# Attention and mixture of experts on one core: the last sequence's exponentials go by HBM, and one unit of shared-expert work moves ahead of the last router

## The chip, the cores and the metric

The kernel runs on one core of a Trainium2 chip. Its metric is the device time of one execution in microseconds (us). Five engines work side by side, each through a queue of its own in a fixed order: TensorE (PE, matmuls and transposes), VectorE (DVE), ScalarE (ACT), GpSimd (POOL) and SyncE (SP, which issues transfers here). An instruction waits until the semaphores that it names have arrived; everything behind it in its queue waits with it. Transfers (DMA) run on 16 DMA engines that all queues share.

## The reference, cut to what matters

Eight sequences of 512 tokens with 256 features, all in float32:

```python
x = x + attention(layernorm(x))          # causal, one head of 256, 8 sequences of 512
h = layernorm(x)
shared = (silu(h @ shared_gate) * (h @ shared_up)) @ shared_down        # inner size 512
probs = sigmoid(h @ router_w.T + routing_bias)                          # 8 experts
scores, indices = top_k(probs, 2); scores /= scores.sum(-1)
for each token and each of its two experts e:
    combined += score * ((silu(h @ gate_w[e]) * (h @ up_w[e])) @ down_w[e])
x = x + shared + combined
```

Each token goes to two of eight experts, so 8192 rows of expert work have to be sorted by expert at run time. No expert tile can start before the last sequence has been routed.

## The kernel before, in words

**Three phases.** The first phase walks over the eight sequences, numbered 0 to 7, and does attention, the second norm and the router for each. The second phase works through the routed rows in tiles of 256 (later 128) rows, each with one expert's weights. The third does the shared expert of sequences 4 to 6, which the first phase left over, and adds everything up.

**Attention of a sequence.** A sequence has four chunks of 128 tokens (`NT = 4`). `scores` (line 437) makes one chunk's masked scores and its exponentials. `attend` (line 458) multiplies the turned exponentials with the values: one matmul for chunk 0, two for chunk 1, three for chunk 2, four for chunk 3. The sums go into PSUM tiles called `av`, DVE adds them to the residual (line 476), takes the statistics (line 172), POOL raises the variance to the power of -1/2 (line 179), and DVE writes the normalized row `hn` (line 325). The pool `ps_o` holds `av` and also the small results of the router (`lT`, `pl`), of the placing (`pp`) and of the shared expert's second layer (`po`). It has two buffers, so each of these waits until the one before the last has been read.

**Two ways to turn a tile.** The exponentials must be turned before the second matmul. Sequences in `SENT` (1 to 6) take the way by HBM: all four chunks' scores are made ahead, at the end of the sequence before; two DMAs store the exponentials, eight load them as 32x32 squares (line 424), and DVE turns these (line 434) into `exTs`, first the tile of chunks 0 to 2 (128x768), then that of chunk 3 (128x512). Sequences 0 and 7 take the other way: scores chunk by chunk inside the attention, and PE transposes (line 463) with ACT copies (line 465). The normalized rows for the router have the same two ways: sequences in `WHOLE` (1 to 5) go by HBM in two halves (lines 371, 377, 384); sequence 7 is in `VIA` but not in `WHOLE`, so its first half goes by HBM and its second by PE (line 340); sequences 0 and 6 go by PE.

**Units.** A shared-expert unit (`shared_beside`, line 564) is half a sequence: four hidden blocks of two matmul groups each (line 578, 16 matmuls), ACT's tanh (line 589), two DVE products for each block (lines 593, 596), and eight matmuls of the second layer (line 605). The list `waiting` holds eight units of sequences 0 to 3, and two of sequence 7 at the end. One unit stands beside each of the sequences 0 to 5, after the next sequence's scores and values; the router of that sequence runs inside it. None stands beside sequence 6, whose router runs at once. One unit is interleaved with sequence 7's attention and router (the call with `halfway=mixed`): its blocks 0 and 1 may go before that attention's last matmul, the others after. Three units are left behind the last router.

**The tail of the first phase.** The router's logits (`lT`, line 492) become probabilities and choices on DVE (lines 504 to 535), `places_of` (line 540) turns them into row numbers `at`, and POOL sends each chunk's rows to HBM by indirect DMA (`dispatch`, line 557, eight DMAs for one sequence). `plan_tiles` (line 189) makes the table of tiles and writes blank rows (line 199). Then SP loads the first tile's rows `h` (line 851), which wait for every dispatched row and blank, DVE turns them into `hTt` (line 873), and PE starts the first expert tile (line 900). ACT issues the expert weights `w` (line 838).

**What sets the order.** The program is written once, in the order that the loops have it; a scheduler then lays out each engine's queue. `tc.issue_after(x)` makes what it holds stand behind `x` where both are on the same engine; it adds no wait. Within these rules the scheduler puts first what it holds to be ready first, and the built queue is fixed from then on.

Of the kernel before, what the change touches and what calls it, by code (L numbers as in the profile page):

```python
# [26 lines left out]
def kernel(  # L27
# [248 lines left out]
    with ExitStack() as first, ExitStack() as inner:  # L276
# [181 lines left out]
        def attend(xb, i, ex, inv, v, mv, rstd, hn, meanwhile=None, exT=None):  # L458
            n = (i + 1) * P
            if exT is None:  # L460
                pt = ps_t.tile([P, S], F32, tag="t", name="pt")
                for j in range(i + 1):
                    nc.tensor.transpose(pt[:, ts(j, P)], ex[:, ts(j, P)], ident)
                exT = work.tile([P, S], F32, tag="exT", name="exT")
                marks["exT"] = nc.scalar.copy(exT[:, :n], pt[:, :n]).ins
            else:
                exT = part(exT, i)
            if meanwhile is not None:
                meanwhile()
            av = ps_o.tile([P, D], F32, tag="o", name="av")  # L470
            for j in range(i + 1):
                mixed = nc.tensor.matmul(  # L472
                    av, lhsT=exT[:, ts(j, P)], rhs=v[:, j, :], start=(j == 0), stop=(j == i)
                )
            with tc.issue_after(marks["turned"]) if "turned" in marks else nullcontext():
                summed = nc.vector.scalar_tensor_tensor(
                    out=xb[:, i, :], in0=av, scalar=inv, in1=xb[:, i, :], op0=ALU.mult, op1=ALU.add
                )
            stats_of(mv, xb[:, i, :], i)
            power = rstd_of(rstd[:, i : i + 1], mv[:, i : i + 1, :])  # L480
            if i:
                with tc.issue_after(summed.ins) if i != NT // 2 or xb is not total[B - 1] else nullcontext():
                    normalize(hn[:, i - 1, :D], xb, i - 1, mv, rstd)
            return mixed.ins, summed.ins, power

        def route(b, hT, hn):
# [22 lines left out]
            for r in range(TOP):  # L509
                top, hot = tops[r][:, here], hots[r][:, here, :]  # L510
                if r:
                    yield
                with tc.issue_after(marks["turned"]) if r and b < B - 2 else nullcontext():
                    nc.vector.tensor_reduce(out=top, in_=prob, axis=AX.X, op=ALU.max)
                nc.vector.tensor_tensor(
                    out=hot, in0=prob, in1=top.unsqueeze(2).to_broadcast(wide), op=ALU.is_equal
# [47 lines left out]
        def shared_beside(b, half, hT, midway=None, behind=None, rows_from=NI, early=None, steps=(), halfway=None):  # L564
# [8 lines left out]
            for m in range(NI):  # L573
                pg = ps_m.tile([P, 2, n], F32, tag="m", name="pg")
                for w in range(2):
# [13 lines left out]
                nc.scalar.activation(sg, pg[:, 0, :], AF.Tanh, scale=0.5)  # L589
# [40 lines left out]
        for b in range(B):  # L630
# [27 lines left out]
            for i in range(NT):  # L658
# [95 lines left out]
            def chosen(b=b, hT=hT, hn=hn):  # L754
# [18 lines left out]
            if b + 1 < B:  # L773
                choice = chosen()
                next(choice)
                if b + 2 == B:
                    for _ in choice:
                        pass
            else:
                added = shared_beside(*waiting.pop(0), early=chosen(), rows_from=0, halfway=mixed, steps=((NI // 2, 1), (NI - 1, 0), (NI - 1, 1)))  # L780
            if b in LATE:
# [3 lines left out]
                waiting += [(b, 0, hT), (b, 1, hT)]  # L785
            if b + 1 < B:

                if b + 2 < B:
                    def behind():

                        nonlocal exT
                        with tc.issue_after(marks["hid"]), tc.issue_after(marks["first"]):
                            exT = turn_exponentials(squares)
                        next(choice, None)
                        marks["squares"], marks["turned"] = marks["turned"], marks["run"]

                    def midway():
                        if b + 3 < B:
                            with tc.issue_after(marks["squares"]):
                                rows, _ = first_norm(*coming)  # L800
                            with tc.issue_after(marks["sent"]):
                                blocks[b + 3], _ = sent_to_blocks(xn_d[b + 3], rows)

                    added = shared_beside(
                        *waiting.pop(0), midway=midway, behind=behind, early=choice,
                        rows_from=1 if b in WHOLE else NI,
                        steps=((NI // 2, 1), (NI - 1, 1)) if b in WHOLE else ((0, 1), (1, 1)),
                    )
                xT = ahead_T
        placed()  # L810
        for c in to_send:
# [316 lines left out]
```

## Time and profile before

| what | value |
|---|---|
| median of 13 runs | 678.18 us (676.97 to 679.32) |
| the profiled execution's own time | 676.17 us |
| its span | 674.4 us |
| PE busy | 663.6 us, 98% of the span |
| DVE, ACT, POOL busy | 301.5, 151.0, 158.0 us |
| first expert matmul starts at | 259.26 us |
| PE's clock as granted | 1.00 in every stretch until PE has finished |

The span is what the profiler records; 1.8 us of the execution's time lie outside it. The median of the runs is 2.01 us above the profiled execution, so a sum made against the profile is carried over by adding 2.01 us.

The lines of a timeline are: start in us, time covered in us, engine, line of the kernel, operation, tile written <- tiles read, shape, and count. Behind them, in brackets, is how long the engine had been idle and what ended that. A float32 matmul counts as two instructions and a transpose by PE as one.

### The profile page before, as it was taken

To read this page: it belongs to the slowest core of one execution; us is meant where nothing else is said; L and a number is where in the kernel's file an instruction comes from. 1 tells how busy PE (TensorE), PEld (TensorE's weight loads), DVE (VectorE), ACT (ScalarE), POOL (GpSimd) and SP (SyncE) were. 2 spreads that over 40 slices of the span, in tenths; PEclk is the share of its full clock that TensorE was granted. 3 is DMA by queue.
4 is the path that set the end of the run, shared out by engine and by line. 5 is a ranking of instruction groups with operands and counts; after the bars stand their busy time and mean duration, and the time that the engine had idled before them with its cause. 6 is when DMAs were issued, how large, how long until landed. Compare 5 with 4: busy or idle time off the path is not lost.

```text
span 674.4 us, 10379 instructions
## 1 busy us (share of the span) xinstructions
PE 663.6 (98%) x3178; PEld 543.4 (81%) x3178; DVE 301.5 (45%) x1002; ACT 151.0 (22%) x359; POOL 158.0 (23%) x210
## 2 busy tenths in 40 slices
PE   7999999999999999999999999999999999999997
PEld 5677777777776888888888888888888899994556
DVE  4668879779776853212212122122122112223765
ACT  2442321332313222121111111211111111111110
POOL 3102451532516520112121111211121112121000
PEclk9999999999999999999999999999999999999999
DMA  7653877767743366967455454453543557824775
GB/s 229 185 140 108 227 211 188 209 185 219 210 120 128 108 174 216 274 175 218 140 174 163 127 181 137 152 180 111 172 160 106 165 164 237 246 91 154 245 222 176
DMA packets 152809, 118.48 MB, mean 176 GB/s; under 512 B 109648, under 2 KB 131280, under 8 KB 152752
## 3 DMA queue, kind: packets, MB, share of 16 engines
q1 hardware_dynamic: 133552, 57.00, 32.5%
q10 hardware_dynamic: 12912, 43.53, 18.6%
q0 software_dynamic: 6288, 17.24, 7.0%
q8 instruction: 28, 0.46, 0.3%
q14 instruction: 29, 0.24, 0.1%
HBM read 82.79 MB, written 34.95 MB: 175 GB/s over the span
## 4 chain that ended last, share of the span: by engine, by line
PE 94%; DVE 1%; DMA 1%; POOL 1%; ACTq 1%; ACT 1%; issue 1%; SPq 0%; DVEq 0%; POOLq 0%
PE po L923 17%; PE pg L900 17%; PE pu L900 17%; PE pg L578 10%; PE po L605 5%; PE av L472 4%; PE sc L442 4%; PE pm L395 4%; PE pm L407 4%; PE pg L1011 3%; PE po L1070 3%; PE pu L1011 3%; PE lT L492 1%; POOL rows_h L559 1%; DMA wk<-in_wk_dram 1%; ACTq L838 1%
## 5 line engine op out<-in xcount | busy, mean ns | idle before, releaser
L886 DVE TENSOR_TENSOR hidp<-pu,sgt 128x512 f32<-128x512 f32 x56 | 38.6, 690 | 209.9 <-PE pu L900 198.9
L929 POOL DMA_INDIRECT rows_y<-y,to x56 | 53.9, 962 | 266.2 <-ACT y L928 143.9
L900 PE MATMUL pg<-hTt,w 128*128 128x256 f32 x448 | 105.9, 379 | 0.1
L900 PE MATMUL pu<-hTt,w 128*128 128x256 f32 x448 | 105.8, 379 | 0.0
L923 PE MATMUL po<-w_down,hidp 128*128 x448 | 101.3, 379 | 0.0
L900 PEld LDWEIGHTS pg<-hTt,w 128*128 128x128 f32 x448 | 85.0, 190 | 12.0 <-ACT sgt L885 0.5
L900 PEld LDWEIGHTS pu<-hTt,w 128*128 128x128 f32 x448 | 85.1, 190 | 11.6
L923 PEld LDWEIGHTS po<-w_down,hidp 128*128 128x128 f32 x448 | 85.0, 190 | 11.5
L578 PE MATMUL pg<-hT,w_sh 128*128 128x256 f32 x320 | 74.0, 383 | 0.2 <-ACT hT L341 0.2
L559 POOL DMA_INDIRECT rows_h<-hn,at x64 | 63.4, 990 | 22.7 <-issue 17.5
L885 ACT ACTIVATE sgt<-pg 128x512 f32<-128x512 f32 x67 | 39.9, 597 | 127.6 <-PE pg L900 120.1
L578 PEld LDWEIGHTS pg<-hT,w_sh 128*128 128x128 f32 x320 | 59.5, 190 | 9.5 <-ACT sg L589 1.0
L928 ACT COPY y<-po 128x256 f32<-128x256 f32 x67 | 24.9, 373 | 150.6 <-PE po L923 145.9
L179 POOL TENSOR_TENSOR rstd<-var,minus_half 128x1 f32<-128x1 f32 (+1 forms) x43 | 27.0, 636 | 125.1 <-DVE var L178 94.2
L442 PE MATMUL sc<-xT,qT 128*128 128x128 f32 (+3 forms) x128 | 37.4, 434 | 0.0
L605 PE MATMUL po<-w_sh,hid 128*128 128x256 f32 x160 | 36.5, 381 | 0.0
L605 PEld LDWEIGHTS po<-w_sh,hid 128*128 128x128 f32 x160 | 29.5, 190 | 5.0 <-DVE hid L596 0.7
L395 PE MATMUL pm<-xT,w_qk 128*128 128x512 f32 x64 | 29.9, 592 | 0.0
L886 DVE TENSOR_TENSOR khid<-pu,sgt 128x512 f32<-128x512 f32 x11 | 7.6, 692 | 48.9 <-PE pu L900 48.9
L407 PE MATMUL pm<-wv_sb,xT 128*128 128x256 f32 x128 | 29.0, 380 | 0.2 <-ACT xT L341 0.2
L407 PEld LDWEIGHTS pm<-wv_sb,xT 128*128 128x128 f32 x128 | 24.2, 190 | 6.2 <-issue 2.6
L172 DVE BATCH_NORM_STATS2 bnst<-total 128x6 f32<-128x256 f32 x64 | 25.2, 410 | 8.1 <-DMA total<-in_x_dram 8.0
(156 smaller groups left out, 757.6 us busy)
## 6 DMA issues: line engine op xcount, KB each, us to landing
w<-in_gate_w_dram ACTq DMA_DIRECT2D x41, 512.0 KB, 3.9
w<-in_up_w_dram ACTq DMA_DIRECT2D x41, 512.0 KB, 4.3
yl<-rows_y SPq DMA_DIRECT2D x32, 256.0 KB, 3.9
h<-rows_h SPq DMA_DIRECT2D x112, 64.0 KB, 3.5
w_down<-in_down_w_dram SPq DMA_DIRECT2D x8, 512.0 KB, 5.3
out_dram<-total SPq DMA_DIRECT2D x32, 128.0 KB, 3.2
total<-in_x_dram SPq DMA_DIRECT2D x7, 512.0 KB
xnd<-xn SPq DMA_DIRECT2D x6, 512.0 KB
```

The source lines that it names most:

```text
L395: nc.tensor.matmul(pm, lhsT=w_qk[:, k, ts(m, P)], rhs=xT[:, k, :], start=(k == 0), stop=(k == ND - 1),)
L407: nc.tensor.matmul(pm, lhsT=xT[:, k, ts(c, P)], rhs=wv_sb[:, k, :], start=(k == 0), stop=(k == ND - 1),)
L442: nc.tensor.matmul(sc[:, :n], lhsT=qT[:, k, ts(i, P)], rhs=xT[:, k, :n], start=(k == 0), stop=(k == ND - 1),)
L559: lands(nc.gpsimd.indirect_dma_start(out=rows_h[:, :], out_offset=bass.IndirectOffsetOnAxis(ap=at[:, r, c : c + 1], axis=0), in_=hn[:, c, ...
L578: mm = nc.tensor.matmul(pg[:, w, :], lhsT=w_sh[:, ds(w * gu + k * I + m * P, P)], rhs=hT[:, k, at], start=(k == 0), stop=(k == ND - 1),)
L605: nc.tensor.matmul(po, lhsT=hid[:, m, ts(j, P)], rhs=w_sh[:, ds(2 * gu + m * D, D)], start=(m == 0), stop=(m == NI - 1),)
L885: nc.scalar.activation(sg, pg, AF.Silu)
L886: return nc.vector.tensor_tensor(out=hid, in0=pu, in1=sg, op=ALU.mult).ins
L900: nc.tensor.matmul(dst[:, m, :], lhsT=w[:, i, k, ts(m0 + m, P)], rhs=hT[:, ts(k, n * P)], start=(k == 0), stop=(k == ND - 1),)
L923: nc.tensor.matmul(po, lhsT=hid[:, m, ts(j, P)], rhs=w_down[:, ds(w + m * D, D)], start=(m == 0), stop=(m == NI - 1),)
L929: nc.gpsimd.indirect_dma_start(out=rows_y[:, :], out_offset=bass.IndirectOffsetOnAxis(ap=to[:, j : j + 1], axis=0), in_=y, in_offset=None,)
L1011: nc.tensor.matmul(dst, lhsT=w_sh[:, ds(off + k * I + m * P, P)], rhs=hT[:, k, :], start=(k == 0), stop=(k == ND - 1),)
```

## The change

Five edits belong together.

1. `SENT` takes in sequence 7. Its four chunks' scores are made ahead, at the end of sequence 6, and its exponentials are stored, loaded and turned by DVE. Ten PE transposes and their four ACT copies go. Since there is no next sequence to project, `project_q` is left out for it.
2. `VIA` and `WHOLE` take in sequence 6 and leave out sequence 7. Sequence 6's normalized rows go by HBM in two halves, in place of eight PE transposes; sequence 7's rows all go by PE, eight transposes in place of four.
3. A unit stands beside sequence 6, with its router inside, as for the sequences before it.
4. The unit at sequence 7 holds back its blocks from block 1 on (before: from block 2 on) until the attention's last matmul.
5. Two units are left behind the last router, in place of three. The number of units as a whole stays the same.

```diff
-    VIA = [b for b in range(1, B) if b != B - 2]
-    WHOLE = range(1, B - 2)
-    SENT = range(1, B - 1)
+    VIA = range(1, B - 1)
+    WHOLE = range(1, B - 1)
+    SENT = range(1, B)
...
-                with tc.issue_after(summed.ins) if i != NT // 2 or xb is not total[B - 1] else nullcontext():
+                with tc.issue_after(summed.ins):
                     normalize(hn[:, i - 1, :D], xb, i - 1, mv, rstd)
...
-                with tc.issue_after(marks["turned"]) if r and b < B - 2 else nullcontext():
+                with tc.issue_after(marks["turned"]) if r and b < B - 1 else nullcontext():
                     nc.vector.tensor_reduce(out=top, in_=prob, axis=AX.X, op=ALU.max)
...
-                    elif (m, w) == (NI // 2 - 1, 1) and halfway is not None:
+                    elif (m, w) == (0, 1) and halfway is not None:
                         held = halfway
...
-                    if i % 2 == 0:
+                    if i % 2 == 0 and ahead_T is not None:
                         with tc.issue_after(mixed) if i else nullcontext():
                             qT = project_q(ahead_T, range(i // 2 * ND // 2, (i // 2 + 1) * ND // 2), qT if i else None)
...
-                if i == (1 if b in SENT else 2) and placed is not None:
+                if i == (1 if b in SENT and ahead_T is not None else 2) and placed is not None:
                     placed()
...
-                if b < B - 2:
+                if b < B - 1:
                     yield
...
                 choice = chosen()
                 next(choice)
-                if b + 2 == B:
-                    for _ in choice:
-                        pass
...
             if b + 1 < B:
-                if b + 2 < B:
-                    def behind():
...
+                def behind():
...
+                added = shared_beside(
+                    *waiting.pop(0), midway=midway, behind=behind, early=choice,
+                    rows_from=1 if b in WHOLE else NI,
+                    steps=((NI // 2, 1), (NI - 1, 1)) if b in WHOLE else ((0, 1), (1, 1)),
+                )
```

More of the change, by code (lines that the diff above doesn't have):

```diff
@@ L786, with midway @@
             if b + 1 < B:
-                if b + 2 < B:
-                    def behind():
[L791 to L808, printed above, removed]
+                def behind():
+                    nonlocal exT
+                    with tc.issue_after(marks["hid"]), tc.issue_after(marks["first"]):
+                        exT = turn_exponentials(squares)
+                    next(choice, None)
+                    marks["squares"], marks["turned"] = marks["turned"], marks["run"]
+                def midway():
+                    if b + 3 < B:
+                        with tc.issue_after(marks["squares"]):
+                            rows, _ = first_norm(*coming)
+                        with tc.issue_after(marks["sent"]):
+                            blocks[b + 3], _ = sent_to_blocks(xn_d[b + 3], rows)
+                added = shared_beside(
[3 more added lines that the diff above has]
+                )
                 xT = ahead_T
```

## The prediction, made before the result was known

> **What bounds the kernel now.** I read the page's busy shares first, then the engines' timelines from 165 to 270 us, since every edit lies there. The page says that PE hardly pauses:
>
> ```profile
> span 674.4 us, 10379 instructions
> PE 663.6 (98%) x3178; PEld 543.4 (81%) x3178; DVE 301.5 (45%) x1002; ACT 151.0 (22%) x359; POOL 158.0 (23%) x210
> ```
>
> So a change can win only PE work or the few pauses, and loses whatever new pause it makes. PE's timeline shows the two ways of a sequence: sequence 6's scores to its first attention matmul (170.67 to 191.40), and sequence 7's, chunk by chunk, from 197.88.
>
> ```profile
> 174.99 3.62 PE L407 MATMUL pm<-wv_sb,xT 128*128 128x256 f32 x16
> 178.44 5.34 PE L578 MATMUL pg<-hT,w_sh 128*128 128x256 f32 x24
> ...
> 189.69 1.88 PE L395 MATMUL pm<-xT,w_qk 128*128 128x512 f32 x4
> 191.40 1.46 PE L472 MATMUL av<-v,exTs 128*128 128x256 f32 x6
> ...
> 204.51 0.33 PE L500 MATMUL pl<-ident,logits 128*128 128x128 f32 x1 [0.39 <-ACT logits L497]
> ...
> 213.30 0.41 PE L545 MATMUL pp<-run,ones 128*128 128x32 f32 x2 [0.33 <-DVE run L535]
> 214.10 0.66 PE L463 MATMUL pt<-ident,ex 128*128 128x128 f32 x4 [0.39 <-ACT ex L451]
> ...
> 222.19 0.64 PE L492 MATMUL lT<-hT,r_sb 128*32 128x128 f32 x16
> ...
> 238.54 7.07 PE L578 MATMUL pg<-hT,w_sh 128*128 128x256 f32 x32
> 245.44 3.62 PE L605 MATMUL po<-w_sh,hid 128*128 128x256 f32 x16
> 248.90 7.07 PE L578 MATMUL pg<-hT,w_sh 128*128 128x256 f32 x32
> 255.80 3.62 PE L605 MATMUL po<-w_sh,hid 128*128 128x256 f32 x16
> 259.26 1.89 PE L900 MATMUL pg<-hTt,w 128*128 128x256 f32 x8
> ```
>
> The pauses shown after 197.88 are 1.3 us in all. The last router starts at 222.19, the first expert tile at 259.26, with no pause between them: 37.07 us. I take the start of the first expert tile as the measure, since PE has no pause from 270 to 600 us and what follows moves with it.
>
> What hides behind these 37.07 us is the dispatch. POOL's last dispatch is issued at 240.98, and the timeline of the DMA queue has the first load of rows soon after it lands:
>
> ```profile
> 246.81 1.95 SPq L851 DMA_DIRECT2D h<-rows_h  x4
> ```
>
> That is 24.62 us after the router's start. The fourth load starts at 248.4; a load there lands 1.9 us after issue; DVE's turn takes 0.67, two hand-overs 0.25 (ACT's exponentials end at 213.95, PE starts at 214.10; DVE's `run` ends at 213.24, PE starts at 213.30). So an expert tile cannot start before 29.1 us after the last router. Today the cover is longer by 8 us.
>
> **PE's own work.** From 197.88 the new order of PE is: all four scores 4.32 (170.67 to 174.99 for sequence 6), values 3.45 (to 178.44), a unit with router 11.25 (to 189.69), then block 0 of the next unit, 1.73 (a quarter of 238.54 to 245.44). That ends at 218.63. Ten `av` matmuls at 0.43 and the placing at 0.37 (194.41 to 194.78) would bring 223.32; then eight matmuls 3.46, eight transposes 0.92 (four took 220.77 to 221.23), two matmuls 0.87: the last router at 228.57 without a pause. Behind it one unit (238.54 to 248.90, 10.36) is gone: 26.71 remain. Sum 255.28 against 259.26, a gain of **3.98**: 14 transposes (about 1.5), the 1.3 of pauses, and the rest start-up between small groups.
>
> **A new wait on DVE.** The built order of the changed kernel puts on DVE, for sequence 7: the first turn of exponentials (768 wide), then both products of block 0 (lines 593, 596), then the second turn (512 wide), then the second half of sequence 6's routing, then the first residual sum. Sequence 6 has no products there:
>
> ```profile
> 189.21 1.57 DVE L434 STREAM_TRANSPOSE exTs<-squares 128x768 f32<-128x768 f32 x2
> 190.71 0.14 DVE L514 TENSOR_REDUCE top<-prob 128x4 f32<-128x32 f32 x1
> ...
> 192.69 0.48 DVE L476 SCALAR_TENSOR_TENSOR total<-av,inv,total 128x256 f32<-128x256 f32 x1
> ```
>
> The products wait for PE's block 0 (218.63) and ACT's tanh. In the tail a block ends at 240.27 and its products run thus:
>
> ```profile
> 240.88 0.42 DVE L593 SCALAR_TENSOR_TENSOR sg<-sg,pg 128x256 f32<-128x256 f32 x1 [1.03 <-ACT sg L589]
> 241.33 0.42 DVE L596 TENSOR_TENSOR hid<-pg,sg 128x256 f32<-128x256 f32 x1
> ```
>
> They end 1.48 after the block: 220.11. The 512-wide turn takes 0.67 (least of line 434): 220.78. From the line 514 that overlaps it by 0.07 to line 476 it is 1.98 (190.71 to 192.69), and 0.48 for the sum: 223.17. PE has done chunks 0 and 1 by 219.93, and chunk 2 needs chunk 0's PSUM buffer (two in the pool): it starts at about 223.25, a pause of **3.3**. Sequence 6 escaped this by a 1.73 us `project_q` between chunks 1 and 2 and by the earlier DVE order.
>
> Chunk 2 ends at 224.55, the placing at 224.92. Chunk 3 needs chunk 2's buffer, and DVE has statistics, POOL's power and a normalize before chunk 2's sum. In sequence 5 the sums of chunks 0 and 2 start 3.32 apart (166.45, 169.77); 0.34 of that is placing work, which now comes later: 2.98. So the sum runs from 225.67 to 226.15, chunk 3 starts at 226.25, a second pause of **1.33**. Bounds for the two: 0 if DVE's order does not bind, 5.7 if chunk 2's sum is 4.02 behind chunk 0's as in sequence 6 (192.69, 196.71). I take 4.65, by the chain that the built order has. The last router then starts at 228.57 + 4.65 = 233.2.
>
> **The cover.** PE would be free at 233.2 + 26.7 = 259.9, the rows are ready at 233.2 + 29.1 = 262.3: a pause of **2.4**. Against 259.26 that is +3.0 us (-3.98 + 4.65 + 2.4).
>
> **What costs nothing, and its cover.** *Exponentials by HBM:* sequence 6's first turn ends at 190.19, 27.21 later 217.4, against 218.63 needed; 1.2 of margin. Landing may be 2.4 slower (6.3 against the usual 3.9), so 0 to 1.2; no gain, as PE does not wait there. I take 0, since the traffic is lighter: no input rows are sent to blocks any more. *SP's queue:* 20 DMAs more (four stores, 16 loads), five fewer, all between 198 and 214 us; its next work, the blanks, comes at about 243. POOL's queue gets none. *Values:* four copies of about 0.37 move from DVE to ACT, which is 22% busy. *Sequence 6's dispatch:* its row numbers come near 228, and eight DMAs at 1.27 apart follow chunk 3's power, about 230.6 to 240.8; sequence 7's first dispatch is due at 242.5 (9.3 after the router). Without that margin of 1.7 each us late is a us on the path. *Second expert tile:* its row loads (260.9 to 262.5) now meet the weight loads that ACT issues from 260.7 on, and ACT's activation for tile 0 stands behind a weight load that waits for the last of these rows. Landing 1.9 (idle queue) to 6.3 (a load at 267.7 amid the weights): activation done by 266.4 or 270.8, wanted at 269.2. Cost 0 to 1.6; at the page's median for such loads, 3.5, it is 0, which I take.
>
> [...] PE's granted clock is 1.00 in every stretch, also in the 2 us after its last matmul; but after 3.97 us of waiting at the start the 256-wide matmuls of line 307 took 500 ns, against 380 later. A pause of 3.3 lies close to that. [...] The last two dispatches landed 6.8 and 5.3 us after issue. [...] The trace decides here for 5.3, as weights and blanks are under way at the same time after the change too.
>
> **The sum.** 676.17 + 3.0 = 679.2 for the profiled execution; the median stands 2.01 above it: **681.2 us**.
>
> **Rivals.** *Faster, by the DVE order:* if the products of block 0 came early enough, both pauses vanish and the dispatch alone binds: 228.57 + 29.1 = 257.7, 676.6. For it: DVE is only 45% busy. Against it: they cannot start before PE's block 0 has ended. It decides only where both pauses together stay under 0.3 us. *Same, by quick landing:* if the dispatches land after 2.4 (the least in the tail) in place of 5.3, the rows are ready before PE: 259.9, that is 678.8. So too if the pauses are 0.3 to 3 us. Against: the same bytes cross in both kernels. *Slower still:* the second tile's wait (1.6), a late exponential (1.2) or a slowed PE: 682.4 to 684. That the change does not do what it says is excluded by the built order: PE has 14 transposes fewer, and all units are there.
>
> **How the numbers follow.** Chances: the forecast's case, 680 to 682.3, 0.65; slower still 0.17; same 0.11; faster 0.07. A measurement of this kernel tells 0.2%, 1.36 us, from no change. The range 678.6 to 683.8 takes in the quick landing and the second tile's and the exponentials' bounds, and leaves out the faster case and the worst tail.
>
> **What would show it.** In the profile after: PE's `av` chunk 2 with 3.3 us idle before it, released by DVE line 476, chunk 3 with about 1.3; the last router 35.3 us after the scores of sequence 7 start (24.3 before); the first expert matmul with an idle of 2 to 3 released by DVE's `hTt`; no PE transposes of `ex` after the first sequence. I am wrong if the first idle is under 1 us, or if rows land before the last unit ends.

## The result and the profile after

The changed kernel takes **689.09 us** (median of 8 runs, 687.32 to 690.83), the kernel before 678.22 us (37 runs beside it): slower, by 10.87 us, a ratio of 1.016 (95% interval 1.0146 to 1.0173). The prediction was 681.2, with a range up to 683.8: the sign was right, the size was not.

The page of the changed kernel, first lines. PE pauses more than before, and has 14 instructions fewer:

```profile
span 689.3 us, 10366 instructions
PE 667.8 (97%) x3164; PEld 545.3 (79%) x3164; DVE 304.1 (44%) x1001; ACT 150.3 (22%) x358; POOL 157.8 (23%) x210
```

PE's timeline of the changed kernel. Lines of the code from 785 on have numbers lower by 4 than before (900 is 896, 885 is 881, 873 is 869, 923 is 919, 838 is 834, 851 is 847):

```profile
201.10 4.48 PE L442 MATMUL sc<-xT,qT 128*128 128x128 f32 x16
...
222.22 1.46 PE L472 MATMUL av<-v,exTs 128*128 128x256 f32 x6
226.78 2.75 PE L472 MATMUL av<-v,exTs 128*128 128x256 f32 x6 [3.10 <-DVE total L476]
...
230.10 2.13 PE L472 MATMUL av<-v,exTs 128*128 128x256 f32 x8
...
237.42 0.65 PE L492 MATMUL lT<-hT,r_sb 128*32 128x128 f32 x16
...
266.35 1.99 PE L896 MATMUL pg<-hTt,w 128*128 128x256 f32 x8 [1.72 <-DVE hTt L869]
...
277.41 3.05 PE L896 MATMUL pg<-hTt,w 128*128 128x256 f32 x8 [3.89 <-ACT sgt L881]
...
621.05 1.97 PE L919 MATMUL po<-w_down,khid 128*128 x8 [1.94 <-issue]
```

Four pauses have appeared: 3.10 us before chunk 2's attention matmuls, 1.72 before the first expert tile, 3.89 before the second, and 1.94 at the run-time branch near the end, where the profile names no releaser ("issue"). A fifth loss shows in durations: six instructions of `av` take 2.75 us in place of the usual 1.46, and the second tile's first eight 3.05 in place of 1.89. The view by windows, cut at the edges of the clock's own records, says why. Its columns are the stretch, its length, busy time and count of PE, PEld, DVE, ACT and POOL, then the granted clock, the DMA share and GB/s:

```profile
223.59:227.00 3.41, 0.31 (x2) 0.22 (x2) 3.10 (x15) 0.00 (x0) 0.00 (x0) 1.00 0.00 0
227.00:230.42 3.42, 3.42 (x11) 2.87 (x11) 2.52 (x11) 0.00 (x0) 1.09 (x2) 0.50 0.00 0
230.42:233.83 3.41, 3.41 (x17) 3.00 (x17) 2.75 (x18) 0.00 (x0) 0.55 (x1) 1.00 0.00 0
...
274.79:278.20 3.41, 0.79 (x4) 0.71 (x5) 1.52 (x3) 2.37 (x3) 0.00 (x0) 1.00 0.99 284
278.20:281.62 3.42, 3.42 (x10) 2.67 (x9) 1.23 (x3) 0.60 (x1) 0.00 (x0) 0.50 1.00 303
```

After a window of 3.41 us in which PE was busy for only 0.31 us, and after one with 0.79, the clock is 0.50 for exactly one window. With PE at work all through it, each costs half of its 3.41 us, 1.7.

**Where the time went**, profile against profile (the spans differ by 14.9):

| stretch | before | after | difference |
|---|---|---|---|
| start to the scores of sequence 7 | 197.88 | 201.10 | +3.2 |
| from there to the first expert matmul | 61.38 | 65.25 | +3.9 |
| second expert tile, pause and half clock | 0 | 3.89 + 1.7 | +5.6 |
| branch near the end | 0 | 1.94 | +1.9 |

The first row is not the change: in the thirteen profiles of the experiments, whose code is all but the same up to there, the scores of sequence 7 start between 199.5 and 203.7 (200.21 and 201.34 in b1 and b2, which have the code of the kernel before up to there). The profile before had an early start (its time is 2.0 below its median) and the one after a late end (2.1 above). The last three rows add up to 11.4, and that is what there is to explain in the 10.87.

### The profile page after: what moved, and what is told of

Its sections match the earlier page's. It is cut to its first block, busy times and chain, and to the rows that moved or that the text cites. A ratio compares the mean times of both kernels' runs of the same rounds, so it can differ in the third digit from the quotient of the medians.

```text
span 689.3 us, 10366 instructions
## 1 busy us (share of the span) xinstructions
PE 667.8 (97%) x3164; PEld 545.3 (79%) x3164; DVE 304.1 (44%) x1001; ACT 150.3 (22%) x358; POOL 157.8 (23%) x210
## 4 chain that ended last, share of the span: by engine, by line
PE 85%; DVE 6%; DMA 4%; SPq 2%; issue 1%; ACT 1%; POOL 0%; ACTq 0%; DVEq 0%
PE po L919 17%; PE pg L896 17%; PE pu L896 16%; PE pg L578 8%; PE av L472 4%; PE sc L442 4%; PE pm L407 3%; PE pg L1007 3%; PE po L605 3%; PE po L1066 3%; PE pu L1007 3%; PE pm L395 2%; DMA w<-in_up_w_dram 1%; SPq L377 1%; SPq L424 1%
## 5 line engine op out<-in xcount | busy, mean ns | idle before, releaser
L472 PE MATMUL av<-v,exTs 128*128 128x256 f32 x140 | 34.7, 395 | 3.1 <-DVE total L476 3.1
L472 PEld LDWEIGHTS av<-v,exTs 128*128 128x128 f32 x140 | 26.7, 196 | 9.6 <-DVE total L476 3.5
L589 ACT ACTIVATE sg<-pg 128x256 f32<-128x256 f32 x40 | 15.4, 384 | 67.8 <-PE pg L578 56.2
```

What stands on the lines that cost most here:

```text
L472: mixed = nc.tensor.matmul(av, lhsT=exT[:, ts(j, P)], rhs=v[:, j, :], start=(j == 0), stop=(j == i))
```

## Experiments

Each run is compared with runs of the kernel before that were taken beside it, whose medians were 679.18, 679.40, 687.06 and 678.20 us; so ratios are compared, with 0.1% being 0.68 us. The changed kernel stands at 1.016. "Half clock" and "branch" are the losses named above. "Cover" is the work that PE has behind the last router while rows are sent and loaded; "tile 0" and "tile 1" are the first and the second expert tile. This table has the pauses of each run's profile, in us, and the windows at half clock before PE had finished:

| run | ratio (95% interval) | before chunks 2, 3 | tile 0 | tile 1 | branch | half clock |
|---|---|---|---|---|---|---|
| the changed kernel | 1.0160 (1.0146 to 1.0173) | 3.10 | 1.72 | 3.89 | 1.94 | 2 |
| r1_sums_first | 1.0107 (1.0088 to 1.0127) | 0.36, 1.02 | 2.17 | 1.73 | 1.92 | 1 |
| r2_two_blocks | 1.0147 (1.0125 to 1.0170) | 3.10 | 2.76 | 1.28 | 1.9 | 2 |
| r4_gate_first | 1.0127 (1.0102 to 1.0153) | 3.10, 0.49 | 2.65 | 0 | 1.44 | 3 |
| r7_one_behind | 1.0100 (1.0085 to 1.0116) | 3.10 | 2.19 | 0 | 1.6 | 2 |
| r5_extra_unit | 1.0183 (1.0162 to 1.0205) | 3.10 | 0 | 0 | 0.22 | 1 |
| b1_unit_moved | 1.0027 (1.0008 to 1.0046) | 0 | 2.60 | 0 | 0 | 1 |
| r6_pad14 | 1.0090 (1.0071 to 1.0110) | 1.58, 1.02 | 3.10 | 0 | 0 | 2 |
| b2_half_moved | 1.0075 (1.0053 to 1.0097) | 0 | 0 | 0 | 1.61 | 0 |
| c3_sums_half | 0.9979 (0.9963 to 0.9995) | 0.35, 1.02 | 0 | 0 | 0 | 0 |
| c3_again | 0.9983 (0.9973 to 0.9993) | 0.35, 1.02 | 0 | 0 | 0 | 0 |
| a1_after_again | 1.0166 (1.0124 to 1.0207) | 3.10 | 1.84 | 3.80 | 1.95 | 6 |
| c5_fills | 1.0026 (1.0013 to 1.0038) | 0.53, 1.03 | 0.55 | 0 | 0 | 1 |
| c6_between | 1.0012 (0.9993 to 1.0032) | 0, 0.21 | 0 | 0 | 0 | 2 |

### The pause before chunk 2: r1_sums_first and r2_two_blocks

DVE's timeline of the changed kernel shows the order that makes the pause. The products of block 0 (lines 593 and 596) wait for ACT's tanh of PE's block 0, the turn and the routing queue up behind them, and the first residual sum (line 476) comes last:

```profile
222.84 0.42 DVE L593 SCALAR_TENSOR_TENSOR sg<-sg,pg 128x256 f32<-128x256 f32 x1 [1.85 <-ACT sg L589]
223.29 0.42 DVE L596 TENSOR_TENSOR hid<-pg,sg 128x256 f32<-128x256 f32 x1
223.63 0.70 DVE L434 STREAM_TRANSPOSE exTs<-squares 128x512 f32<-128x512 f32 x1
...
226.25 0.48 DVE L476 SCALAR_TENSOR_TENSOR total<-av,inv,total 128x256 f32<-128x256 f32 x1
```

r1 puts both products behind the last residual sum:

```diff
-                    marks["half"] if m >= rows_from else marks["coming"]
+                    first if first is not None and m == 0 else marks["half"] if m >= rows_from else marks["coming"]
...
-                added = shared_beside(*waiting.pop(0), early=chosen(), rows_from=0, halfway=mixed, steps=((NI // 2, 1), (NI - 1, 0), (NI - 1, 1)))
+                added = shared_beside(*waiting.pop(0), early=chosen(), rows_from=0, halfway=mixed, first=summed, steps=((NI // 2, 1), (NI - 1, 0), (NI - 1, 1)))
```

> The changed kernel with one order added on DVE: both products of the last unit's block 0 stand behind the last residual sum of sequence 7, so that the sums no longer wait for PE's block 0 and ACT's tanh. Theory (the 3.10 us pause before chunk 2's av and the 3.41 us at half clock behind it lie on the path): the last router comes 4 to 5.2 us earlier after the scores of sequence 7 (36.3 in the changed kernel), the first expert tile moves by as much, and the time is 684 to 685.5. Rival A (the rows are bound by the dispatch of sequence 6 on POOL's queue and not by the last router): the router is earlier, the pause before the first expert tile is longer by as much, 688 to 689. Rival B (the products held back make PE wait for block 0's buffer instead): a new pause of 2 to 3 us in the unit, 687 to 689.

Measured: 686.46, ratio 1.0107, 3.6 us under the changed kernel. PE's timeline of r1:

```profile
222.05 1.56 PE L472 MATMUL av<-v,exTs 128*128 128x256 f32 x6 [0.36 <-DVE total L476]
...
225.00 1.99 PE L472 MATMUL av<-v,exTs 128*128 128x256 f32 x8 [1.02 <-DVE total L476]
...
232.19 0.64 PE L492 MATMUL lT<-hT,r_sb 128*32 128x128 f32 x16
...
261.55 1.99 PE L896 MATMUL pg<-hTt,w 128*128 128x256 f32 x8 [2.17 <-DVE hTt L869]
...
270.45 1.99 PE L896 MATMUL pg<-hTt,w 128*128 128x256 f32 x8 [1.73 <-ACT sgt L881]
```

The last router comes 32.69 us after the scores (199.50), 3.63 earlier than in the changed kernel, the first tile is 3.2 nearer to them, and the time falls by 3.6: the pause lies on the path, and rivals A and B fall. The move was expected to be 4 to 5.2; chunk 3's own pause of 1.02, which the half clock had covered, comes to light. That 3.2 and 3.6 agree so well is in part luck: the profile is of r1's fastest run (683.91), in which tile 1 loses only 1.73, with no half clock, and the pause at the branch brings a half clock instead.

r2 undoes edit 4:

```diff
-                    elif (m, w) == (0, 1) and halfway is not None:
+                    elif (m, w) == (NI // 2 - 1, 1) and halfway is not None:
```

> The changed kernel with edit 4 undone: blocks 0 and 1 of the last unit may go before the last attention matmul, as before the change, in place of block 0 alone. DVE's built order then has the products of both blocks ahead of the first residual sum. Theory (the pause before chunk 2 is DVE standing behind products that wait for PE's blocks; edit 4 only says how many): the pause stays at about 3.1 us, since the products that the sum stands behind come later by as much as PE has more to do, and the time is that of the changed kernel within 1 us, 688 to 690. Rival (edit 4 itself opened the pause, since block 1 no longer fills it): the pause falls under 1.5 us and the time to 685 to 686.5.

Measured: 689.28, ratio 1.0147, and the pause is 3.10 again: the theory holds, and edit 4 did no harm. More PE work ahead only puts off what DVE stands behind.

### The cover: r5_extra_unit and b1_unit_moved

r5 computes the last unit a second time behind the router and does not add that result:

```diff
+        again = waiting[-1]
         while waiting:
             shared_beside(*waiting.pop(0))()
+        shared_beside(*again)
```

> The changed kernel with one unit more behind the last router: the last unit is computed a second time and this second result is not added, which leaves the output as it was and adds 10.36 us of PE work (one unit of the profile before). Theory (the cover behind the last router is what both pauses at the expert tiles lack): the 1.7 us before the first tile and the 5.6 us of pause and half clock at the second go, 689.1 + 10.4 - 1.7 - 5.6 = 692.1, bounds 691 to 694. Rival (the pauses have other causes, such as the second tile's loads against each other, at whatever time they run): the second pause stays and only the first goes, 697.8; or neither goes, 699.4.

Measured: 691.56, ratio 1.0183: 1.5 us more than the changed kernel for 10.36 us more work, so 8.8 us of losses have gone: 7.3 at the two tiles, as the theory has it, and 1.7 at the branch, whose pause is 0.22 here. PE's timeline of r5, from the last unit into the second tile, has no idle time at all:

```profile
270.69 3.62 PE L605 MATMUL po<-w_sh,hid 128*128 128x256 f32 x16
274.14 1.89 PE L898 MATMUL pg<-hTt,w 128*128 128x256 f32 x8
...
281.05 1.89 PE L898 MATMUL pg<-hTt,w 128*128 128x256 f32 x8
```

b1 goes the other way: the kernel before, with one unit less behind the router.

```diff
                 if b + 2 == B:
                     for _ in choice:
                         pass
+                    added = shared_beside(*waiting.pop(0))
```

> The kernel before with one edit alone: one of the three units behind the last router stands beside sequence 6, behind its router; the exponentials and rows of sequences 6 and 7 stay on their old ways. Theory (cover alone makes the pauses at both expert tiles): 26.7 us of cover against 28.9 until the rows are turned gives 2.2 at the first tile, and the second tile costs 5.6 as in the changed kernel: 678.2 + 2.2 + 5.6 = 686.0, bounds 684.5 to 687. Rival A (as predicted, the first tile's rows alone): 680.4. Rival B (the second tile's pause comes from the exchanges of sequence 7 by HBM and not from the cover): 680 to 681, with under 1 us of pause at the second tile.

Measured: 680.73, ratio 1.0027. PE's timeline of b1:

```profile
262.37 3.62 PE L901 MATMUL pg<-hTt,w 128*128 128x256 f32 x8 [2.60 <-DVE hTt L874]
265.82 1.89 PE L901 MATMUL pu<-hTt,w 128*128 128x256 f32 x8
...
271.00 1.89 PE L901 MATMUL pg<-hTt,w 128*128 128x256 f32 x8
```

The first tile's pause is there as foreseen, with a half clock behind it (3.62 for 1.89), but the second tile has none, and the time is that of rival A and of rival B alike. b1 does not part the two; r5 speaks against B, since sequence 7's exchanges by HBM are all in it and the second pause is gone. Less cover is thus not enough for the second pause by itself: here tile 0 was slowed by 1.7 us, and its activation ran 5.1 us after the first expert matmul (267.46), against 10.4 in the changed kernel. Why the loads landed sooner here (2.2 to 6.2 us after issue) is not shown.

### The second tile: r4_gate_first and r7_one_behind

The timeline of the changed kernel at the second tile, SP, ACT and DVE together (SPq and ACTq are the engines' DMA issues):

```profile
264.78 2.18 SPq L847 DMA_DIRECT2D h<-rows_h  x4
265.24 0.38 ACTq L834 DMA_DIRECT2D w<-in_gate_w_dram  x1
...
272.14 0.34 ACTq L834 DMA_DIRECT2D w<-in_gate_w_dram  x1
275.10 0.34 ACTq L834 DMA_DIRECT2D w<-in_up_w_dram  x1
275.16 0.71 DVE L869 STREAM_TRANSPOSE hTt<-h 128x512 f32<-128x512 f32 x1 [8.29 <-DMA h<-rows_h]
275.47 1.28 ACT L881 ACT_TABLE_LOAD   x1 [10.42 <-DMA h<-rows_h]
...
276.76 0.60 ACT L881 ACTIVATE sgt<-pg 128x512 f32<-128x512 f32 x1
```

The rows of tile 1 and the weights of tiles 1 and 2 are issued within 3.5 us (264.78 to 268.2). The rows, issued by 266.96, are turned at 275.16; the trace gives the loads of rows issued here 5.5 to 7.5 us to land. ACT's queue has tile 3's weight loads ahead of tile 0's activation, and these two are held until 272.14 and 275.10; so the activation that frees PSUM for tile 1 ends at 277.36, with PE done since 273.5.

In the kernel before, the activation stood behind the same weight loads, but nothing came late:

```profile
249.85 1.85 SPq L851 DMA_DIRECT2D h<-rows_h  x4
...
257.22 1.29 DVE L873 STREAM_TRANSPOSE hTt<-h 128x512 f32<-128x512 f32 x2
...
264.45 1.28 ACT L885 ACT_TABLE_LOAD   x1 [4.61 <-DMA w<-in_up_w_dram]
```

Tile 1's rows were issued at 249.85, ten us before the first of these weights (260.03), and were turned together with tile 0's at 257.22; the activation ran at 265.75, 6.5 us after the first expert matmul.

r4 fetches weights and rows of tiles 2 and 3 behind the activation, r7 those of tile 3 alone:

```diff
-            nc.scalar.activation(sg, pg, AF.Silu)
+            marks["sgt"] = nc.scalar.activation(sg, pg, AF.Silu).ins
...
-            if t + AHEAD <= MEAN:
+            if t and t + AHEAD <= MEAN:
...
+            if t == 0:
+                with tc.issue_after(opening), tc.issue_after(marks["sgt"]):
+                    items += [fetch(s)[1] for s in range(AHEAD, AHEAD + 1)]
```

(In r4 the last line has `range(2, AHEAD + 1)`, and the first fetches stop at tile 1.)

> The changed kernel with the weights and rows of tiles 2 and 3 fetched only behind ACT's activation of tile 0, so that this activation does not stand behind weight loads that wait for the rows of tile 1. Theory (the 3.89 us pause before the second expert tile is ACT held in its queue by weight loads, and the half clock follows from the pause): pause under 1 us there, no stretch at half clock behind it, 683.5 to 685. Rival (the rows of tile 1 themselves land late, 8.4 us after issue, since the dispatch and the blanks are still under way): DVE's turn for tile 1 stays at 11 us after the first expert matmul, the pause is still over 2.5 us, 688 to 689.

Measured: 687.89, ratio 1.0127, 2.2 us under the changed kernel; the two intervals overlap, so this is not clear of noise. The pause at the second tile is gone, as the theory has it, but the time fell less than expected: this profile has three windows at half clock, two of them at chunks 2 and 3, one at the first tile behind a pause of 2.65.

> The changed kernel with the weights and rows of tile 3 alone fetched behind ACT's activation of tile 0; those of tile 2 are fetched where they were. The activation then has no weight load ahead of it in ACT's queue that waits for rows of tile 1, while tile 1's rows still share the DMA engines with the weights of tiles 1 and 2. Cause A (ACT's queue holds the activation): the activation runs as soon as PE's gate matmuls are done, about 3.6 us after the first expert matmul (10.4 in the changed kernel's profile), and the pause before the second expert tile falls under 1 us. Cause B (the rows themselves land late, since they are issued together with two sets of weights): DVE's turn for tile 1 stays at 8 to 9 us after the first expert matmul, and the pause stays at 1.5 to 3 us. Time by A 2 to 4 us under the changed kernel, a ratio of 1.010 to 1.013 to the kernel before; by B 0.5 to 1.5 us under it, 1.013 to 1.016.

Measured: 684.87, ratio 1.0100, 4.1 us under the changed kernel. Timelines of r7, PE's first and ACT's next:

```profile
265.28 3.21 PE L896 MATMUL pg<-hTt,w 128*128 128x256 f32 x8 [2.19 <-DVE hTt L869]
...
273.98 1.89 PE L896 MATMUL pg<-hTt,w 128*128 128x256 f32 x8
```

```profile
268.68 1.28 ACT L881 ACT_TABLE_LOAD   x1 [5.17 <-DMA w<-in_gate_w_dram]
269.98 0.60 ACT L881 ACTIVATE sgt<-pg 128x512 f32<-128x512 f32 x1
```

The activation runs 4.7 us after the first expert matmul, and there is no pause at the second tile: cause A, ACT's queue, by time and by pause. But cause B is there too. DVE's turn for tile 1 still starts 7.2 us after the first expert matmul (272.51; 8.8 in the changed kernel), and tile 0 was long here, 8.7 us, for its half clock. With tile 0 at its usual 6.9 the rows would have been late by about 1 us. So the queue made most of the pause; that the rows alone make about 1 us is worked out, not run.

The missing pause alone would not show the queue, since its size varies: r1 and r2, whose code at this place is the changed kernel's, have 1.73 and 1.28 without a half clock, where the two profiles of the changed kernel have 3.89 and 3.80. What shows it is when the activation starts, counted from the first expert matmul: 7.8 to 10.4 us in these four profiles, 4.7 in r7, 3.6 in r4. In c5 (below), which has r4's order and tile 0 at full clock, it is 2.0, and tile 1 starts without a pause 7.0 us after tile 0.

### Half clock and branch: r6_pad14

r6 puts 14 PE transposes that nobody reads into the pause before chunk 2:

```diff
+                if b == B - 1 and i == NT // 2:
+                    spare = ps_t.tile([P, S], F32, tag="t", name="spare")
+                    with tc.issue_after(mixed):
+                        for _ in range(14):
+                            fill = nc.tensor.transpose(spare[:, :P], ident, ident).ins
...
+                with tc.issue_after(fill) if b == B - 1 and i == NT // 2 else nullcontext():
                     mixed, summed, power = attend(...)
```

> The changed kernel with 14 PE transposes added whose result nobody reads, in the pause before chunk 2's attention matmuls of sequence 7. They take 1.5 us, so the last router does not move by them. Two claims: (a) the clock is halved for 3.41 us when PE has been idle for about 1.9 us or more of one of the 3.41 us windows that the clock's records show; with 1.5 of the 3.1 us filled no window has that, so the half clock at chunk 2 goes, -1.3 to -1.7; (b) the 1.94 us without a cause at the branch to the last down matmuls is PE's code arriving late, which goes by where the branch lies in PE's code; 14 instructions are what PE has fewer than in the kernel before, so the branch lies where it lay before and the pause goes, -1.9. Theory with both: 685.5 to 686.5; with (a) alone 687.5; with (b) alone 687; with neither 689 to 690.

Measured: 685.54, ratio 1.0090: 14 instructions more make the kernel 4.7 us faster. The two timelines of PE in r6 that the claims speak of:

```profile
222.76 1.69 PE L678 MATMUL spare<-ident 128*128 128x128 f32 x14
226.03 1.56 PE L472 MATMUL av<-v,exTs 128*128 128x256 f32 x6 [1.58 <-DVE total L476]
...
614.54 3.62 PE L926 MATMUL po<-w_down,khid 128*128 x16
```

(a) Chunk 2 starts no earlier, but at full clock (1.56 for six). (b) The 16 last down matmuls run on without a pause at the branch. Over all runs of r6 the mean granted clock was 0.995 to 1.000, median 0.998, against 0.992 to 0.998, median 0.994, of the changed kernel; 0.0025 of it is one window of half clock in 690 us, 1.7 us. By that, 1.9 for the branch and about 2.7 for the clock would make up the 4.7.

The profiled run shows the branch's part, but not that the clock's part comes from chunk 2. The first expert matmul starts 65.75 us after the scores, against 65.25 in the changed kernel. The pause before tile 0 is 3.10 here, and two windows at half clock follow it (265.82 to 272.65); tile 0 is so slow by them, 10.04 us, that tile 1 does not wait, and the first four tiles take 41.12 us, against 43.93. Here the gain is thus 1.9 at the branch and 2.8 at the first tiles, and where the other runs have theirs stays open.

That the pause at the branch goes with the number of PE instructions is shown across the table: 1.4 to 1.95 in all six profiles with the changed kernel's 3164 PE instructions (the changed kernel twice, r1, r2, r4, r7), 0 in all four with 3178 (before, b1, r6, c5), 0 with 3196 (c3 twice, c6), 0.22 with 3212 (r5) and 1.61 with 3210 (b2). c5 is the sharpest case: r1's and r4's edits, which alone leave the pause, and 14 transposes, with which it is gone. That the count matters through the place of the branch in PE's code, and that PE waits for code to be loaded, is argued only: the trace has loads of 16 KB on a queue for instructions, taken here to be PE's, and one began at 617.72 and the next at 621.05, when PE went on; in the profile before they began at 601.81 and 605.09, with PE at work on both sides of the branch, which lies at 606.2 there.

### Both losses had back: c3_sums_half, b2_half_moved, c3_again, c6_between

c3 keeps the change and gives the cover back without more work. It has the sums first as in r1, and one half of sequence 6's shared expert is a unit behind the last router, in place of the last phase:

```diff
+                if b == LATE[-1]:
+                    waiting.append((b, 0, hT))
...
+        some = ds(S // 2, S // 2) if b == LATE[-1] else ds(0, S)
...
-                        dst, lhsT=w_sh[:, ds(off + k * I + m * P, P)], rhs=hT[:, k, :],
+                        dst[:, some], lhsT=w_sh[:, ds(off + k * I + m * P, P)], rhs=hT[:, k, some],
...
-        for c in range(NT):
+        for c in range(NT // 2 if b == LATE[-1] else 0, NT):
```

> The changed kernel with two edits: the products of block 0 behind the last residual sum, as in the run r1_sums_first, and one half of sequence 6's shared expert as a unit behind the last router in place of the last phase; the work as a whole is the same, the cover behind the router is 10.4 us longer. Theory (the losses are the DVE order and the lost cover, and both can be had back): 691.56 of the run with an extra unit, less the unit's 10.36, less 3.6 for the sums, 677.6 against 679.2 of the kernel before in the same call, -1.6, bounds -4 to 0. Rival (the last phase, 10 us shorter, no longer hides its loads and sums): 2 to 6 us above the kernel before.

Measured: 677.71, ratio 0.9979 (0.9963 to 0.9995). PE's timeline of c3 has only DVE's small waits left, no window at half clock, and no pause at the branch:

```profile
223.44 1.56 PE L472 MATMUL av<-v,exTs 128*128 128x256 f32 x6 [0.35 <-DVE total L476]
...
226.39 1.99 PE L472 MATMUL av<-v,exTs 128*128 128x256 f32 x8 [1.02 <-DVE total L476]
...
270.96 1.89 PE L898 MATMUL pg<-hTt,w 128*128 128x256 f32 x8
```

The sum from r5 and r1 said 677.6. The control has the moved half without the change:

> The kernel before with one half of sequence 6's shared expert as a unit behind the last router in place of the last phase, and nothing else: a control for the run c3_sums_half. Theory (the kernel before has cover enough, so more of it is worth nothing): same as before within 0.7 us. Rival (the moved half is itself a gain or a loss by the last phase): 1.5 us or more from it, on either side.

Measured: 684.33, ratio 1.0075: its rival. Its profile (682.89) stands 6.7 above that of the kernel before: 3.5 by the start, 1.61 by a pause at the branch, 1.6 in the last stretch, where 5.1 us pass between PE's end and the end of the span (3.5 before). So the moved half is no gain of its own: without the change it loses. The start varies between executions (the scores of sequence 7 at 199.5 to 203.7 in the thirteen profiles); what of its 3.5 is chance stays open. The profiled run had a mean clock of 1.000, but three of the six runs had 0.994 or 0.995: they lose time at half clock in places that this profile does not show.

> The kernel of the run c3_sums_half once more, the same code. If its gain holds, the ratio to the kernel before is 0.996 to 1.000 again. If the code's pauses on the chip of the last three runs (2.8 to 4.1 us before the last placing, which ACT's late copies release) belong to the chip, they show here too when it is the same chip, and the ratio is 1.000 to 1.003.

Measured: 677.31, ratio 0.9983 (0.9973 to 0.9993), on another chip than the first time. Both intervals lie below 1: c3 is faster than both kernels, by 0.2%.

c6 is c3 with block 1 between chunks 1 and 2 (`halfway=(marks["second"], mixed)`, with `held = halfway[m]` after each of the first two blocks), and the products of two blocks behind the last normalize.

> The kernel of the run c3_sums_half with block 1 of the last unit between chunk 1's and chunk 2's attention matmuls, and the products of blocks 0 and 1 behind the last normalize of sequence 7. Theory (behind this router the cover is 8 us longer than the rows need, so only PE's own pauses count, and 0.35 + 1.02 of them can be filled): 677.7 - 1.4 = 676.3. Rivals: PE waits for the last normalize instead, with one block less behind the attention, 677.7; or the branch's place in PE's code brings its pause back, 679.

Measured: 687.82, ratio 1.0012 (0.9993 to 1.0032). Chunk 3's pause fell to 0.21, chunk 2's went, but the ratio is no better than c3's; it fell on the chip of a1 and c5, where the kernel before took 687.06 and a pause of 3.88 us before the last placing stood in the profile. Whether c6 is worth more than c3 is open.

### Sums: c5_fills and a1_after_again

c5 is r1 and r4 together, with the 14 transposes between the last unit and the first expert tile. No work is moved.

> The changed kernel with three edits and no work moved: the sums first as in r1_sums_first, the later weights behind tile 0's activation as in r4_gate_first, and 14 PE transposes that nobody reads between the last unit and the first expert tile. Theory (the losses add): 686.5 of the run with the sums first, less 1.7 at the second tile, less 1.9 at the branch, which lies again where it lay before the change, less 1.2 of half clock, since the 2.2 us before the first tile fall to 0.7: 681.7, bounds 680.5 to 683. Rival (what is removed at one place comes back at the next): 684 or more.

Measured: 688.39, ratio 1.0026 (1.0013 to 1.0038); 681.7 to 679.2 would have been 1.0037. The losses add: of the 1.66% that the change costs beside these runs (a1, next), these three edits have 1.4 back, with all of the change still in it.

> The changed kernel once more, for a second profile of the same code. What belongs to the code should come back: 3.1 us before chunk 2's av, 1.4 to 2 us at the branch to the last down matmuls, and pauses at the first two expert tiles whose sum is 4 to 6 us. What hangs on where the clock's windows of 3.41 us lie in this execution may differ: which of the pauses a half clock follows, and the start, so that the scores of sequence 7 begin anywhere from 199.5 to 201.3. Time 1.6 per cent above the kernel before, 689 to 691. Rival (the pause at the branch is chance): it is under 0.3 us here.

Measured: 697.82, ratio 1.0166 (1.0124 to 1.0207). The waits of PE in this profile:

```profile
PE pg L896 <- ACT sgt L881: 3.8, 1, 3.8
PE av L472 <- DVE total L476: 3.1, 1, 3.1
PE pp L544 <- DVE mask L530: 2.8, 1, 2.8
PE po L919 <- issue: 1.9, 1, 1.9
PE pg L896 <- DVE hTt L869: 1.8, 1, 1.8
```

All four pauses come back within 0.15 us, the branch too, so none of them is chance. What was not expected is the chip: the scores start at 203.65, and there is a pause of 2.8 us before the last placing (4.1 in c5, 3.9 in c6, 0.3 elsewhere), with ACT's copies of line 609 idle for 5 to 7 us before it and no releaser in the trace that names a line. It belongs to that chip or that time; the ratio did not change by it.

## Why the prediction was wrong, and where it was right

- **PE's own work, -3.98: nearly right.** 57.4 us were foreseen from the scores of sequence 7 to the first expert matmul, without pauses. The changed kernel has 65.25, less pauses of 3.10, 1.72 and 0.6 and 1.7 of half clock: 58.1.
- **The new wait on DVE, 4.65: right in place, nearly in size.** 3.10 for 3.3 before chunk 2, released by line 476, by the chain foreseen. Chunk 3's 1.33 measured 1.02, but only in runs where no half clock covered it. The last router came 36.32 us after the scores (35.3 foreseen).
- **The cover, 2.4: right.** 28.93 us from the last router to the first expert matmul (29.1 foreseen), and a pause of 1.72; 2.17 to 3.10 in the profiles where the second pause was smaller or gone and nothing filled the first (r1, r2, r4, r7, b1, r6). From the end of the last dispatch's issue to the first load of rows 5.0 us passed (256.73 to 261.72; 4.9 before): the trace's price for a landing held, not the 2.4 of the rival (the last dispatch landed 5.43 us after issue, 5.31 before).
- **The second expert tile, 0, with bounds 0 to 1.6: this is the step that failed.** It costs 3.89, and 1.7 more by the half clock behind it. The mechanism was named, ACT's activation behind a weight load that waits for rows. The size was wrong in two places. The rows' landing was bounded by 6.3 us, from a load at 267.72 whose nearest weight load was 2.6 us ahead of it; among four weight loads issued within 2.0 us (265.24 to 267.22) it was 5.5 to 7.5. And the queue held not one weight load but two in turn, 272.14 and 275.10, and the table load of 1.28 behind them: the activation was done 11.0 us after the first expert matmul, where the worst case had 8.5. r7 shows that it is this queue. With this step the measure failed too: the prediction took the start of the first expert tile and let everything behind it move along, but from there to the branch 354.70 us passed, against 346.99 before.
- **The clock: weighed, and dropped.** The prediction held its pause of 3.3 us against the 3.97 of waiting at the start, behind which 256-wide matmuls took 500 ns in place of 380, and its sum has nothing for it. The pauses cost 2.3 windows in a run of the changed kernel on average (mean clock 0.9943 over ten runs, some of it after PE has finished), near 4 us. An idle time as long as that at the start was not needed: the pause of 3.10 before chunk 2 brought a half clock, and so did one of 1.92 in r1.
- **Not in the prediction at all:** 1.94 us at the branch, which came with 14 PE instructions fewer.
- **The rivals.** "Slower still" was the right one, and its bounds of 682.4 to 684 were too tight, since its mishaps were not independent: with the cover given back neither expert pause is there (r5), and a pause can bring a half clock, as one of 1.92 us did in r1 (one of 1.94 in the changed kernel did not).

The sum, redone with what was measured: -3.3 (57.4 became 58.1) + 3.1 + 0.6 + 1.7 + 1.7 for the path to the first tile, 3.9 + 1.7 for the second, 1.9 for the branch: 11.3, against the 10.87 between the medians.

## What to carry to other kernels

When cover shrinks, price the second item of a pipeline too, by the whole queue that its first release stands in: what was spread over time before was then issued within 3.5 us here. Price a PE pause of 2 to 4 us at 1.7 us more than its length, and at up to twice that where a second window at half clock follows, as at tile 0 of r6: an estimate from these profiles, where of 17 pauses of 2.17 to 4.1 us behind PE's first 10 us 15 brought a half clock, ten of them one window and five of them two, and those of 2.17 in r1 and 2.76 in r2 brought none. And look at whether a neighbour's work or even idle transposes can break it up. Work that can be done at any time belongs behind the wait with the longest chain, here the last router, and not beside a sequence that has no need of it.

## What the runs showed of the hardware

**The granted clock changed by whole windows.** In all fifteen profiles the stretches of granted clock, until PE has finished, are whole multiples of 3.413 us (215.04 is 63 of them), on a grid whose phase differs between executions. A window at full clock in which PE was busy for 1.49 us or less was followed by a half clock, with two exceptions at 1.41 (the window in which PE finished) and 1.44 (r2); one with 1.57 or more (a1) was not. At half clock a window with 2.92 us of work or less was followed by another (r2, r4, r6, c6 and a1), one with 3.07 or more (r1) was not. Counted at full clock these 2.92 and 3.07 are 1.46 and 1.54 us of work, near the 1.49 and 1.57 above. So a pause of 2.17 us was free in r1, where the grid cut it, as the windows of r1 show:

```profile
257.75:261.17 3.42, 1.62 (x8) 1.09 (x6) 0.39 (x1) 0.77 (x2) 0.00 (x0) 1.00 0.55 84
261.17:264.58 3.41, 3.03 (x14) 2.70 (x15) 0.90 (x2) 0.00 (x0) 0.00 (x0) 1.00 0.92 321
...
609.33:612.74 3.41, 1.49 (x8) 1.01 (x7) 0.59 (x4) 0.37 (x1) 0.96 (x1) 1.00 0.06 18
612.74:616.15 3.41, 3.07 (x8) 1.91 (x6) 0.00 (x0) 0.17 (x1) 0.00 (x0) 0.50 0.09 30
```

The 1.92 us at the branch of the same run fell into one window and cost a half clock.

**Fewer instructions can cost time.** 14 PE instructions fewer came with 1.94 us at a branch, and with 14 that do nothing it was gone again (r6, 4.7 us faster than the changed kernel as a whole). The traces of both kernels have 28 loads of 16,384 bytes each on one queue for instructions. That the branch waits for such a load is not shown: the two loads around it lie 3.3 us apart both in the kernel before, which has no pause there, and in the changed one.
